# Attention scores on 32-row tiles of the array, banks shared with values' results, and a recurrent layer's weights loaded early

## The chip, the core and the metric

The kernel runs on one core of one Trainium2 chip. The core has a matrix engine (TensorE, PE in the profile), a vector engine (DVE), a scalar engine that evaluates functions (ACT), a general engine (POOL), and SyncE (SP), which here only issues transfers. Each engine works through its own instructions in order and waits on semaphores for the others. PE writes its results to PSUM, which has eight banks of 128 partitions x 512 float32 values; DVE and ACT read them from there, and POOL works on SBUF alone.

The metric is the device time of one execution in microseconds (us). Times of several runs are given as a median.

## The reference

The inputs are `x` and a context `ctx`, each 32 batches x 64 tokens x 256 features in float32. Four layers follow each other:

```
x = L0(x, ctx)        # 8 x 64-row channel attention: energies, softmax, values, 64x64 weights, relu
x = L1(x, ctx, ...)   # transformer layer: self attention, cross attention with ctx, gelu MLP
x = L2(x, ctx, ...)   # the same with other weights
x = L3(x, ctx)        # recurrent layer: token shift, mixes, decay, a scan over tokens, gate, feed-forward
```

The attention of L1 and L2 has 16 heads of 16 features:

```
scores = einsum('bhqd,bhkd->bhqk', q, k) / sqrt(16)
scores = scores * mask - 10000.0 * (1.0 - mask)
probs  = softmax(scores, axis=-1)
ctx    = einsum('bhqk,bhkd->bhqd', probs, v)
```

The MLP is `gelu(ln(x) @ w1 + b1) @ w2 + b2` with 1024 hidden features. L3 computes, for every token, `out = r @ (u * k v' + s)` and `s = k v' + w * s` on 8x8 states of 32 heads.

## The kernel before

The 2048 tokens are cut into four groups of 512 (eight batches). A group has four units of 128 tokens (two batches), numbered j = 0 to 3. All of `x` stays in SBUF.

**Order.** Each layer's work on a group is a list of small pieces with a cost (`attention`, `mlp_half`, `recurrent`). `timed` spreads a list over an interval of a made-up time axis, `emit` sorts the pieces of all lists by that time and records their instructions. The intervals come from the constants in `PARAMS`. So the cross attention of one group runs beside the projections of the next, and beside the MLP of groups that are further on. After that a scheduler of the language sets the final order of every engine's queue with its own estimate of the times; `at_once` asks it to keep a set of matmuls together. What stands in the queues is fixed from then on.

**One unit of attention** passes through these pieces (lines of the kernel before):

- `spread` (L388): eight transfers on SP's queue put the keys of a half group into `kbd`. Every head has 16 partitions, and a matmul takes 64 partitions, which hold four heads. So that each head meets only its own keys, `kbd` has four planes, and head h is non-zero in plane h % 4 alone.
- `scores` (L423): eight matmuls, for two feature halves c, two row halves r and two batches h. Each multiplies 64 rows of the transposed queries with 64 x 256 of `kbd` (4 planes x 64 keys), on a 64x64 tile of the array. The result is in two banks, one for each r. Then, for each r, DVE multiplies with the mask into SBUF (L447), POOL adds the mask's second term (L452), DVE takes the maximum over keys (L455), and DVE (r = 0) or POOL (r = 1) subtracts it (L456).
- `turn` (L459): eight transposes on PE (L467), four for each r, and ACT's exp of the turned scores (L471).
- `heads` (L473): 32 small matmuls with the values and a column of ones, into one bank `pc`. DVE takes the reciprocal of the sums (L494) and multiplies (L496) into `cn`.
- `turn_back` (L500): two transposes of `cn` into one bank `pcT`, which ACT and DVE split into a high and a low part (`split`, L179 and L180) for the output product.
- `out` (L512): the product with the output weights, added to `x` by DVE (L199).

The pieces of successive units are interleaved: scores of unit i, turn and heads of i - 1, turn_back of i - 2, out of i - 3.

**Banks.** `bank` hands out the eight banks by tag: two for products ("mm"), two for scores ("sc"), two for turned scores ("tp"), one for values' results ("pc") and one for the turned-back results ("pd"). A new tile of a tag waits until the oldest tile of that tag has been read. The MLP's output (`out_rows_of`) takes "pc" for all but the first group. Layer 0's energies take "sc" and "tp" in turn, its values "pc" and "pd". The recurrent layer uses the same pool.

**The change of phase.** Two SBUF pools of the first layers ("lw", "lp") end, and the recurrent layer's pool ("r") takes their place. Its `load` puts each weight into that pool, by default with a transfer issued on ACT's queue; `load_w` does so on SP's queue. Then the recurrent pieces start, together with the MLP of L2's later groups (`late`).

Of the kernel before, what the change touches and what calls it, by code (L numbers as in the profile page):

```python
# [23 lines left out]
P = 128  # L24
# [7 lines left out]
XM = 32  # L32
# [48 lines left out]
def tile_xattn_stack(ctx: ExitStack, tc: tile.TileContext, a: dict, out: bass.AP):  # L81
# [4 lines left out]
    small = ctx.enter_context(tc.tile_pool(name="small", bufs=4))  # L86
    psum = ctx.enter_context(tc.tile_pool(name="psum", bufs=2, space=PSUM))
    dram = ctx.enter_context(tc.tile_pool(name="dram", bufs=2, space=bass.MemoryType.DRAM))
    work = ctx.enter_context(tc.tile_pool(name="work", bufs=2))
# [4 lines left out]
    def bank(name, tag="mm"):  # L94
        return psum.tile([P, 512], FP, tag=tag, name=name, bufs=BUFS[tag])

# [130 lines left out]
    def layer0(pool):  # L227
# [32 lines left out]
        def energy(g, j):  # L260
# [3 lines left out]
            nmx = small.tile([P, 2, 2], FP, tag="nmx", name=f"nmx_{g}_{j}")  # L264
            att = pool.tile([P, 4, E], FP, tag="s", name=f"att_{g}_{j}", bufs=3)
            for h in range(2):
                pe = bank(f"pe_{g}_{j}_{h}", "sc" if v else "tp").rearrange("p (c m) -> p c m", c=2)
                hs = slice(h * S, (h + 1) * S)
                for c in range(2):
                    nc.tensor.matmul(  # L270
                        pe[:, c, :], st[g][hs, j, c * P : (c + 1) * P], kx[hs, v, :], start=True, stop=True
                    )
                nc.vector.tensor_reduce(nmx[:, h, :], pe, AX.X, ALU.max, negate=True)
                for c in range(2):
                    nc.scalar.activation(
                        att[:, 2 * h + c, :], pe[:, c, :], AF.Exp, bias=nmx[:, h, c : c + 1],
                        accum_out=rs[:, h, c : c + 1],
                    )
# [68 lines left out]
    def attention(stage, key, g, pool, ctx_of, w, mask_of):  # L347
# [75 lines left out]
        def scores(j):  # L423
            kbd, toff = st["kbd", j // 2], (j % 2) * P
            m, n = st["mask"]
            s = st["s", j] = pool.tile([P, 2, NH // 2, S], FP, tag="s", name=f"s_{tag}_{j}", bufs=3)
            banks = [bank(f"psc_{tag}_{j}_{r}", "sc") for r in range(2)]

            mms = []
            for c in (1, 0):  # L430
                for r in (1, 0):
                    rs_ = slice(r * S, (r + 1) * S)
                    for h in range(2):
                        toks = slice((2 * j + h) * S, (2 * j + h + 1) * S)
# [10 lines left out]
            for r in range(2):  # L445
                hs = slice(r * 8, r * 8 + 8)
                nc.vector.tensor_tensor(  # L447
                    s[:, r], banks[r].rearrange("p (h k) -> p h k", k=S),
                    m(j).unsqueeze(1).broadcast_to([P, 8, S]), ALU.mult,
                )  # L450
# [22 lines left out]
        def heads(j):  # L473
            pT, vts = st["pT", j], st["vts", j // 2]
            pc = bank(f"pc_{tag}_{j}", "pc")

            pcp = pc[:, : 17 * NH].rearrange("p (l n e) -> p n l e", l=2, n=8)

            mms = []
            for k in (4, 5, 6, 7, 0, 1, 2, 3):  # L480
                n = 4 * (k // 2 % 2) + 2 * (k // 4) + k % 2

# [17 lines left out]
        def turn_back(j):  # L500
            ps = bank(f"pcT_{tag}_{j}", "pd")
            for c in range(2):
# [42 lines left out]
    def mlp_half(stage, tag, g, u, w, brow):  # L545
# [337 lines left out]

    wts = {}

    with tc.tile_pool(name="lw", bufs=1) as wp, tc.tile_pool(name="lp", bufs=2) as pool:
        m1 = wp.tile([P, S], FP, name="m1")
# [152 lines left out]
        for i, L in enumerate(("L1", "L2")):  # L1040
# [29 lines left out]
    with tc.tile_pool(name="r", bufs=2, reuse_waits="tile") as pool:  # L1070
        c3 = {}

        def load(name, shape, src, eng=nc.scalar):
            c3[name] = pool.tile(shape, FP, name=name, bufs=1)
            eng.dma_start(c3[name], src)

        def load_w(*names):
            for n in names:
                load(n, [P, 2, E], a["w3"][W3[n]].rearrange("(c p) n -> p c n", p=P), nc.sync)

# [6 lines left out]

        load("mw1", [P, 2, 5 * XM], a["maa_w1"].rearrange("(c p) n -> p c n", p=P))
        load("mw2a", [P, E], a["maa_w2"][:P])
        load("mw2b", [XM, E], a["maa_w2"][P:])  # L1090
        load("step", [P, P], a["step"])
        load("st01", [P, 2, B, 2], a["st01"])
        load("dw1", [P, 2, 64], a["decay_w1"].rearrange("(c p) n -> p c n", p=P))
        hold("fx")
        hold("dfx")
        load("avg", [P, P], a["avg"])
        hold("x5", 3)
# [7 lines left out]
        hold("dx")  # L1105
        load_w("Wv", "Wr", "Wk")
        shifted_ring("vsh")

        load("sel", [P, 2, P], a["sel"])
        load("dw2", [64, E], a["decay_w2"])  # L1110
        hold("ta", 1, [P, RR + S])
# [106 lines left out]
```

## Time and profile before

| | |
|---|---|
| median of 3 runs | 1105.0 us (1099.04, 1106.01, 1105.0) |
| the profiled execution, its time | 1094.72 us |
| the profiled execution, its span on the core | 1092.9 us |
| mean granted TensorE clock in it | 0.964 |
| layer 0 | 0 to 109 us |
| L1: self attention, cross attention, rest of the MLP | 109 to 232, 232 to 347, 347 to 427 us |
| L2: self attention, cross attention | 427 to 575, 575 to 705 us |
| recurrent layer with the rest of L2's MLP | 705 to 1093 us |

How to read it: busy time is the time in which an engine executes. A row of the profile has the line of the kernel, the engine, the operation, the tile written and the tiles read, the shape, and the number of instructions; buffer numbers are left out, so `psc_L1c` stands for all score tiles of cross attention in L1, `pc_` for values' results, `ppT_` for turned scores, `pcT_` for turned-back results, `pf_` and `pfo_` for the MLP's products. A float32 matmul stands as two rows. PEld rows are weight loads, which overlap matmuls. In a timeline row the first number is the start, the second the time to the end of the last instruction of the row; brackets give idle time of that engine before it and what ended it.

### The profile page before, as it was taken

The page shows a single profiled execution, that of the slowest core. Times are in us where ns is not written, and L with a number is a line of the kernel's source. Part 1 is how long each engine was busy: PE and PEld are TensorE (multiplying, and loading weights), DVE is VectorE, ACT ScalarE, POOL GpSimd, SP SyncE. Part 2 cuts the span into 40 slices and gives each one's busy share as a digit, 9 for nine tenths or more (in the row PEclk, how much of TensorE's full clock was granted, in tenths as well). Part 3 has the DMA queues.
Part 4 walks back from the last instruction along what each step waited for, and adds up shares of the span by engine and source line. Part 5 has one row for each costly group of instructions (what it writes and reads, how often), then busy time and mean ns, then how long its engine had stood idle before and what let it go on. Part 6 is the DMA issues. An engine that isn't in the chain of part 4 may idle for free.

```text
span 1092.9 us, 26229 instructions
## 1 busy us (share of the span) xinstructions
PE 978.1 (89%) x10690; PEld 770.5 (70%) x10690; DVE 836.6 (77%) x1497; ACT 556.1 (51%) x1287; POOL 548.4 (50%) x568
## 2 busy tenths in 40 slices
PE   6898999999989999989989999889889998869757
PEld 3555776777778989877767678778678777647536
DVE  4986788777877654777688877647898987997983
ACT  4664554554556634864454455444355464346234
POOL 4354776667757344656577755434434533323300
PEclk9999999999999999989999999999999999989879
DMA  9100011111110101141111110033113121530300
GB/s 292 48 21 19 20 44 38 36 26 25 30 22 6 40 1 21 45 137 34 28 41 26 26 22 30 7 93 89 41 49 89 41 58 40 135 79 21 97 10 30
DMA packets 46364, 53.43 MB, mean 49 GB/s; under 512 B 16562, under 2 KB 40484, under 8 KB 44196
## 3 DMA queue, kind: packets, MB, share of 16 engines
q1 hardware_dynamic: 38756, 48.55, 17.0%
q10 hardware_dynamic: 7488, 3.20, 1.2%
q8 instruction: 85, 1.39, 0.5%
q14 instruction: 35, 0.29, 0.1%
HBM read 38.86 MB, written 4.21 MB: 39 GB/s over the span
## 4 chain that ended last, share of the span: by engine, by line
DVE 38%; PE 36%; ACT 8%; POOL 7%; DMA 5%; issue 4%; SPq 2%; ACTq 0%; POOLq 0%; DVEq 0%
DVE vb_r L784 6%; DVE vb_r L769 5%; PE pf_L1m L188 4%; PE pfo_L1m L188 3%; POOL s_L2c L452 2%; PE pfo_L2m L188 2%; PE pf_L2m L188 2%; DVE x L199 2%; POOL s_L1c L452 2%; SPq L392 2%; PE px_r L671 1%; DMA vb_r<-vd_r 1%; DVE x_r L675 1%; DVE s_L1c L447 1%; PE pq_L2c L188 1%
## 5 line engine op out<-in xcount | busy, mean ns | idle before, releaser
L678 POOL TENSOR_TENSOR x_r<-x_r,xn_r 128x512 f32<-128x512 f32 x40 | 60.5, 1521 | 90.9 <-DVE x_r L675 88.4
L784 DVE TENSOR_TENSOR_SCAN vb_r<-wsh,vb_r 128x512 f32<-128x512 f32 x64 | 77.0, 1260 | 5.3 <-ACT wsh L682 5.3
L188 PE MATMUL pf_L2m<-lnT_L2m,w_L 128*128 128x256 f32 x384 | 57.6, 305 | 7.1 <-DVE lnT_L2m L180 5.2
L188 PEld LDWEIGHTS pf_L2m<-lnT_L2m,w_L 128*128 128x128 f32 x384 | 51.9, 204 | 11.1 <-DVE lnT_L2m L180 5.8
L452 POOL TENSOR_TENSOR s_L1s<-s_L1s,n 128x512 f32<-128x512 f32 x32 | 42.5, 1343 | 29.0 <-DVE s_L1s L447 26.1
L452 POOL TENSOR_TENSOR s_L2s<-s_L2s,n 128x512 f32<-128x512 f32 x32 | 43.0, 1359 | 27.5 <-DVE s_L2s L447 27.4
L188 PE MATMUL pfo_L2m<-w_L,hT_L2m 128*128 128x256 f32 x384 | 55.2, 292 | 1.6 <-DVE hT_L2m L570 1.5
L452 POOL TENSOR_TENSOR s_L2c<-s_L2c,n_L2c 128x512 f32<-128x512 f32 x32 | 41.6, 1319 | 29.2 <-DVE s_L2c L447 28.2
L188 PE MATMUL pfo_L1m<-w_L,hT_L1m 128*128 128x256 f32 x384 | 54.5, 289 | 1.6 <-POOL hT_L1m L569 0.8
L188 PE MATMUL pf_L1m<-lnT_L1m,w_L 128*128 128x256 f32 x384 | 52.0, 288 | 3.9 <-ACT hf_L1m L566 1.2
L452 POOL TENSOR_TENSOR s_L1c<-s_L1c,n_L1c 128x512 f32<-128x512 f32 x32 | 41.2, 1307 | 24.3 <-DVE s_L1c L447 24.1
L188 PEld LDWEIGHTS pf_L1m<-lnT_L1m,w_L 128*128 128x128 f32 x384 | 47.6, 191 | 7.2 <-ACT hf_L1m L566 2.1
L188 PEld LDWEIGHTS pfo_L2m<-w_L,hT_L2m 128*128 128x128 f32 x384 | 48.9, 191 | 4.7 <-DVE hT_L2m L570 1.9
L188 PEld LDWEIGHTS pfo_L1m<-w_L,hT_L1m 128*128 128x128 f32 x384 | 49.3, 191 | 3.4 <-POOL hT_L1m L569 1.0
L569 POOL TENSOR_SCALAR hT_L1m<-hf_L1m 128x512 fp32r<-128x512 f32 x32 | 21.8, 682 | 55.5 <-ACT hf_L1m L566 53.8
L570 DVE TENSOR_TENSOR hT_L1m<-hf_L1m,hT_L1m 128x512 fp32r<-128x512 f32 x32 | 25.3, 791 | 30.2 <-POOL hT_L1m L569 30.1
L566 ACT ACTIVATE hf_L1m<-pf_L1m,b_L 128x256 f32<-128x256 f32 x64 | 26.6, 471 | 42.3 <-PE pf_L1m L188 39.9
L133 PE MATMUL pa_r<-vb_r,sel 128*32 128x256 f32 x256 | 22.8, 487 | 28.0 <-DVE vb_r L769 25.7
L569 POOL TENSOR_SCALAR hT_L2m<-hf_L2m 128x512 fp32r<-128x512 f32 x32 | 26.0, 816 | 43.0 <-ACT hf_L2m L566 42.9
L566 ACT ACTIVATE hf_L2m<-pf_L2m,b_L 128x256 f32<-128x256 f32 x64 | 26.6, 470 | 35.2 <-PE pf_L2m L188 27.3
L769 DVE TENSOR_TENSOR vb_r<-vb_r,ksh 128x2048 f32<-128x2048 f32 x16 | 39.3, 2468 | 6.2 <-DMA vb_r<-vd_r 6.2
L675 DVE SCALAR_TENSOR_TENSOR x_r<-px_r,vecs,sx_r 128x256 f32<-128x256 f32 x80 | 34.1, 473 | 7.2 <-PE px_r L671 6.3
(383 smaller groups left out, 3087.2 us busy)
## 6 DMA issues: line engine op xcount, KB each, us to landing
vb_r<-vd_r SPq DMA_DIRECT2D x16, 1024.0 KB
raw_w_L<-in_L_w_dram SPq DMA_DIRECT2D x4, 1024.0 KB
y<-in_y_dram SPq DMA_DIRECT2D x8, 256.0 KB
x<-in_x_dram SPq DMA_DIRECT2D x8, 256.0 KB
ctxT_L1c<-in_yT_dram SPq DMA_DIRECT2D x4, 512.0 KB
kbd<-kT_L1s SPq DMA_DIRECT2D x64, 32.0 KB
kbd<-kT_L1c SPq DMA_DIRECT2D x64, 32.0 KB
kbd<-kT_L2s SPq DMA_DIRECT2D x64, 32.0 KB
```

Source lines behind the costliest of these rows:

```text
L133: return lambda: nc.tensor.matmul(ps, sta, mov, start=start, stop=stop)
L188: nc.tensor.matmul(ps, sta[x], mov[y], start=(at == 0), stop=(at == n - 1))
L199: nc.vector.tensor_tensor(xs, xs, ps, ALU.add)
L392: nc.sync.dma_start(st["kbd", hg][hs, :, h % 4, :], st["kT"][hs, :, hg * 2 * P : (hg + 1) * 2 * P])
L452: nc.gpsimd.tensor_tensor(s[:, r], s[:, r], n(j).unsqueeze(1).broadcast_to([P, 8, S]), ALU.add)
L566: nc.scalar.activation(raw[:, i], ps[:, i], AF.Gelu_apprx_tanh, bias=w()["b1"][:, 2 * f2 + i : 2 * f2 + i + 1])
L569: nc.gpsimd.tensor_scalar(h[:, 0], raw, 1.0, 0.0, ALU.mult, ALU.add)
L570: nc.vector.tensor_tensor(h[:, 1], raw, h[:, 0], ALU.subtract)
L675: nc.vector.scalar_tensor_tensor(d[:, c], ps[:, c], vec("L3_maa_stack", 2 * m + c), sx_("x", c), ALU.add, ALU.mult)
L678: nc.gpsimd.tensor_tensor(d, d, st["x"], ALU.add)
L769: nc.vector.tensor_tensor(v, v, x.unsqueeze(1).broadcast_to([P, 4, 2 * RR]), ALU.mult)
L784: nc.vector.tensor_tensor_scan(v[:, d], flat(st["wsh"]), v[:, d], 0.0, ALU.mult, ALU.add)
```

## The change

Scores: `kbd` gets two planes, and a matmul takes 32 partitions (two heads) and 128 columns (2 planes x 64 keys). There are 16 for a unit, on 32x64 tiles, and each of the four row quarters q writes a bank of its own. The two banks of q = 2, 3 are one tile of tag "b", those of q = 0, 1 one of tag "a", with one buffer each. The mask's multiply reads two banks in one instruction.

Banks: "sc", "pc" and "pd" go. Values' results (`heads`) take the first bank of an "a" tile, turned-back results (`turn_back`) that of a "b" tile; so "a" and "b" each serve scores and results in turn. Layer 0's energies of a unit take one "a" or "b" tile, its values "tp". The MLP's output takes "tp" before the recurrent phase and "pc" in it, for all but the first group. The recurrent layer gets a PSUM pool of its own with the old tags.

Weights: twelve of the recurrent layer's arrays are loaded by `load_early` into the pool that lasts for the whole kernel, at time 4.0 of the made-up axis, on SP's queue. The other six stay at the change of phase, all on SP's queue. The kernel is built with `dynamic_dma_scratch_size=1024`.

```diff
+    def two_banks(name, tag):
+        return psums["two"].tile([P, 2, 512], FP, tag=tag, name=name, bufs=1)
...
+            pes = two_banks(f"pe_{g}_{j}", "ab"[v])
             for h in range(2):
-                pe = bank(f"pe_{g}_{j}_{h}", "sc" if v else "tp").rearrange("p (c m) -> p c m", c=2)
+                pe = pes[:, h].rearrange("p (c m) -> p c m", c=2)
...
-            pr = bank(f"pr_{g}_{j}", "pc" if j % 2 else "pd")
+            pr = bank(f"pr_{g}_{j}", "tp")
...
-                    st["kbd", hg][hs, :, h % 4, :], st["kT"][hs, :, hg * 2 * P : (hg + 1) * 2 * P]
+                    st["kbd", hg][hs, :, h % 2, :], st["kT"][hs, :, hg * 2 * P : (hg + 1) * 2 * P]
...
-            banks = [bank(f"psc_{tag}_{j}_{r}", "sc") for r in range(2)]
+
+            banks = [two_banks(f"psc_{tag}_{j}_{r}", "ab"[r])[:, :, :256] for r in range(2)]
 
             mms = []
             for c in (1, 0):
-                for r in (1, 0):
-                    rs_ = slice(r * S, (r + 1) * S)
+                for q in (3, 2, 1, 0):
+                    qs = slice(q * 32, (q + 1) * 32)
                     for h in range(2):
                         toks = slice((2 * j + h) * S, (2 * j + h + 1) * S)
                         ktoks = slice(toff + h * S, toff + (h + 1) * S)
                         mms.append(mm(
-                            banks[r][h * S : (h + 1) * S, c * 256 : (c + 1) * 256].rearrange(
-                                "p (i k) -> p i k", i=4),
-                            st["qT"][rs_, c, toks], kbd[rs_, c, :, ktoks],
+                            banks[q // 2][h * S : (h + 1) * S, q % 2, c * P : (c + 1) * P].rearrange(
+                                "p (i k) -> p i k", i=2),
+                            st["qT"][qs, c, toks], kbd[qs, c, :, ktoks],
                         ))
...
-            pc = bank(f"pc_{tag}_{j}", "pc")
+            pc = two_banks(f"pc_{tag}_{j}", "a")[:, 0]
...
-            ps = bank(f"pcT_{tag}_{j}", "pd")
+            ps = two_banks(f"pcT_{tag}_{j}", "b")[:, 0]
...
-                st["ps"] = bank(f"pfo_{tag}", "pc" if g else "mm").rearrange("p (j n) -> p j n", j=2)
+                st["ps"] = bank(f"pfo_{tag}", ("pc" if stage == 5 else "tp") if g else "mm").rearrange(
+                    "p (j n) -> p j n", j=2)
...
+    def load_to(pool, name, shape, src):
+        c3[name] = pool.tile(shape, FP, name=name, bufs=1)
+        nc.sync.dma_start(c3[name], src)
+
+    def load_early():
+
+        load_to(const, "step", [P, P], a["step"])
+        load_to(const, "mw1", [P, 2, 5 * XM], a["maa_w1"].rearrange("(c p) n -> p c n", p=P))
+        load_to(const, "st01", [P, 2, B, 2], a["st01"])
+        load_to(const, "mw2a", [P, E], a["maa_w2"][:P])
+        load_to(const, "mw2b", [XM, E], a["maa_w2"][P:])
+        for n in ("Wv", "Wr", "Wk"):
+            load_to(const, n, [P, 2, E], a["w3"][W3[n]].rearrange("(c p) n -> p c n", p=P))
+        load_to(const, "dw1", [P, 2, 64], a["decay_w1"].rearrange("(c p) n -> p c n", p=P))
+        load_to(const, "dw2", [64, E], a["decay_w2"])
+
+        load_to(const, "sel", [P, 2, P], a["sel"])
+        load_to(const, "avg", [P, P], a["avg"])
...
-        env["kbds"] = ring(wp, "kbd", [P, 2, 4, GR // 2], 3, blank)
+        env["kbds"] = ring(wp, "kbd", [P, 2, 2, GR // 2], 3, blank)
...
+        plan.append([(4.0, load_early)])
         emit(*plan)
...
-        def load(name, shape, src, eng=nc.scalar):
-            c3[name] = pool.tile(shape, FP, name=name, bufs=1)
-            eng.dma_start(c3[name], src)
+        def load(name, shape, src):
+            load_to(pool, name, shape, src)
```

More of the change, by code (lines that the diff above doesn't have):

```diff
@@ L87, in tile_xattn_stack @@
     psum = ctx.enter_context(tc.tile_pool(name="psum", bufs=2, space=PSUM))
+    psums = {"mm": psum}
     dram = ctx.enter_context(tc.tile_pool(name="dram", bufs=2, space=bass.MemoryType.DRAM))
@@ L94, in bank @@
     def bank(name, tag="mm"):
-        return psum.tile([P, 512], FP, tag=tag, name=name, bufs=BUFS[tag])
+        return psums[tag].tile([P, 512], FP, tag=tag, name=name, bufs=BUFS[tag])
+    def two_banks(name, tag):
+        return psums["two"].tile([P, 2, 512], FP, tag=tag, name=name, bufs=1)
     x_rows = a["x"].rearrange("(g j p) n -> g p j n", g=NG, p=P)
@@ L447, in scores @@
                 nc.vector.tensor_tensor(
-                    s[:, r], banks[r].rearrange("p (h k) -> p h k", k=S),
-                    m(j).unsqueeze(1).broadcast_to([P, 8, S]), ALU.mult,
+                    s[:, r].rearrange("p (q h) k -> p q h k", q=2), banks[r].rearrange("p q (h k) -> p q h k", k=S),
+                    m(j).unsqueeze(1).unsqueeze(1).broadcast_to([P, 2, 4, S]), ALU.mult,
                 )
@@ L474, in heads @@
             pT, vts = st["pT", j], st["vts", j // 2]
-            pc = bank(f"pc_{tag}_{j}", "pc")
+            pc = two_banks(f"pc_{tag}_{j}", "a")[:, 0]
             pcp = pc[:, : 17 * NH].rearrange("p (l n e) -> p n l e", l=2, n=8)
             mms = []
-            for k in (4, 5, 6, 7, 0, 1, 2, 3):
-                n = 4 * (k // 2 % 2) + 2 * (k // 4) + k % 2
+            for k in (6, 7, 0, 1, 2, 3, 4, 5):
+                n = 4 * (k % 2) + k // 2
                 for q in range(4):
@@ L881, in recurrent @@
         return first, second, third
-    wts = {}
-    with tc.tile_pool(name="lw", bufs=1) as wp, tc.tile_pool(name="lp", bufs=2) as pool:
+    wts, c3 = {}, {}
+    def load_to(pool, name, shape, src):
[13 more added lines that the diff above has]
+        load_to(const, "avg", [P, P], a["avg"])
+    with (
+        tc.tile_pool(name="lw", bufs=1) as wp, tc.tile_pool(name="lp", bufs=2) as pool,
+        tc.tile_pool(name="psum_l", bufs=2, space=PSUM) as pp,
+    ):
+        psums["two"] = psums["tp"] = pp
         m1 = wp.tile([P, S], FP, name="m1")
@@ L1065, in tile_xattn_stack @@
             plan.append([(load, load_mlp("L2"))] if i == 0 else [(MLP_LOAD, load_mlp("L1"))])
+        plan.append([(4.0, load_early)])
         emit(*plan)
-    with tc.tile_pool(name="r", bufs=2, reuse_waits="tile") as pool:
-        c3 = {}
-        def load(name, shape, src, eng=nc.scalar):
-            c3[name] = pool.tile(shape, FP, name=name, bufs=1)
-            eng.dma_start(c3[name], src)
+    with (
+        tc.tile_pool(name="r", bufs=2, reuse_waits="tile") as pool,
+        tc.tile_pool(name="psum_r", bufs=2, space=PSUM, reuse_waits="tile") as pp,
+    ):
+        for tag in ("sc", "tp", "pc", "pd"):
+            psums[tag] = pp
+        def load(name, shape, src):
+            load_to(pool, name, shape, src)
         def load_w(*names):
             for n in names:
-                load(n, [P, 2, E], a["w3"][W3[n]].rearrange("(c p) n -> p c n", p=P), nc.sync)
+                load(n, [P, 2, E], a["w3"][W3[n]].rearrange("(c p) n -> p c n", p=P))
         def hold(tag, bufs=2, shape=None):
@@ L1086, in shifted_ring @@
             c3[name] = ring(pool, name, [P, 2, RB, S], 2, lambda t: nc.gpsimd.memset(t[:, :, :, 0], 0.0))
[L1088 to L1093, printed above, removed]
         hold("fx")
         hold("dfx")
-        load("avg", [P, P], a["avg"])
         hold("x5", 3)
@@ L1105, in tile_xattn_stack @@
         hold("dx")
-        load_w("Wv", "Wr", "Wk")
         shifted_ring("vsh")
-        load("sel", [P, 2, P], a["sel"])
-        load("dw2", [64, E], a["decay_w2"])
         hold("ta", 1, [P, RR + S])
@@ L1206 @@
     from concourse.bass_utils import run_bass_kernel_spmd
-    nc = bacc.Bacc("TRN2", target_bir_lowering=False, num_devices=1)
+    nc = bacc.Bacc("TRN2", target_bir_lowering=False, num_devices=1, dynamic_dma_scratch_size=1024)
     arrays, aps = {}, {}
```

## The prediction

> **What bounds the kernel now.** I read the page's head and chain first, then busy time by stage, then the score blocks on the timeline, and last the change of phase near 710 us.
>
> ```profile
> span 1092.9 us, 26229 instructions
> ...
> PE 978.1 (89%) x10690; PEld 770.5 (70%) x10690; DVE 836.6 (77%) x1497; ACT 556.1 (51%) x1287; POOL 548.4 (50%) x568
> ...
> DVE 38%; PE 36%; ACT 8%; POOL 7%; DMA 5%; issue 4%; SPq 2%; ACTq 0%; POOLq 0%; DVEq 0%
> ```
>
> PE is nearly full, yet the chain that ended last is shared between DVE and PE. The stages differ: the two transformer layers run from 109 to 705 us, the recurrent layer from 705 on, with its DVE scans setting the pace from 760. One steady group of cross attention (busy time in a window):
>
> ```profile
> core 0: us, PE busy (x) PEld busy (x) DVE busy (x) ACT busy (x) POOL busy (x), PEclk, DMA share, GB/s
> 260.40:288.40 28.00, 25.37 (x445) 20.04 (x444) 23.78 (x50) 14.68 (x39) 20.37 (x20) 1.00 0.13 30
> ```
>
> Of 28.0 us PE is busy 25.4, idle 2.6, and DVE is busy 23.8, or 85%. Taking work off PE helps only as long as DVE, which serves its queue in order, answers in time.
>
> **Scores on PE.** The timeline of PE shows two forms of one unit's scores (128 queries):
>
> ```profile
> 235.88 1.11 PE L133 MATMUL psc_L1c<-kbd,qT_L1c 64*64 64x256 f32 x16
> 236.91 1.70 PE L188 MATMUL po_L1s<-wo_L,cT_L1s 128*128 128x256 f32 x12
> ...
> 239.94 1.08 PE L133 MATMUL psc_L1c<-kbd,qT_L1c 64*64 64x256 f32 x8
> 240.95 1.09 PE L467 MATMUL ppT_L1c<-ident,s_L1c 128*128 128x128 f32 x8
> 241.97 1.08 PE L133 MATMUL psc_L1c<-kbd,qT_L1c 64*64 64x256 f32 x8
> ```
>
> A whole unit (8 matmuls, two rows each, on four 64x64 tiles) takes 1.03 us to the start of the next work. Half a unit, on only two tiles, takes 1.01. So tiles do run side by side, and a block costs its rows per tile: four of 0.215 us each, and about 0.17 to get going. Adding up, along the timeline, the time from every scores row to the next start on PE gives 22.8, 19.8, 22.3 and 19.8 us for L1s, L1c, L2s, L2c: 84.6 us.
>
> The change has 16 matmuls of 128 columns on eight 32x64 tiles. A tile still sees four rows, of 128 columns; the transposes' rows of 128 columns start 0.109 us apart. A block is then 4 x 0.109 + 0.17 = 0.60 us. But the built program splits nearly every unit: its halves wait for different banks, and PE's order holds 121 blocks, 114 of them halves and 7 whole. A half costs as much as a whole, so the stages need 121 x 0.60 = 72.6 us: **-12.0**. In a steady group, where units were whole, it is even a loss (four at 1.03 against eight at 0.60); the gain comes from units that were cut up before. Bounds: -14.5 if a block starts 0.02 us sooner; +40 if 32-row tiles do not overlap, which no row shows either way (a half would cost 1.03).
>
> [...]
>
> Values' results lose nothing and stand together: before, five of 64 blocks were cut by scores, costing some 1.7 us over the usual 0.70 each: **-1.7** (0 to -2).
>
> **What the sharing costs.** Before, a unit's scores needed only the multiply of the unit before (L447). Now bank pair "a" passes from the scores' first half (r = 0) to values' results and back, "b" from the second half to the turned-back results. In the new DVE order the reciprocal and normalising product (L494, L496), which free "a", stand behind the maximum and subtraction of the scores just made. So a loop closes through POOL. Its rows, from the steady group's timelines of DVE and POOL:
>
> ```profile
> 261.55 1.29 DVE L447 TENSOR_TENSOR s_L1c<-psc_L1c,m_L1c 128x512 f32<-128x512 f32 x2 [0.16 <-PE psc_L1c L133]
> ...
> 265.04 0.65 DVE L455 TENSOR_REDUCE mx_L1c<-s_L1c 128x8 f32<-128x512 f32 x1
> ...
> 265.70 0.23 DVE L494 RECIPROCAL ris_L1c<-pc_L1c 128x16 f32<-128x16 f32 x1
> 265.84 0.63 DVE L456 TENSOR_TENSOR s_L1c<-s_L1c,mx_L1c 128x512 f32<-128x512 f32 x1
> 266.38 0.41 DVE L496 TENSOR_TENSOR cn_L1c<-pc_L1c,ris_L1c 128x256 f32<-128x256 f32 x1
> ```
> ```profile
> 262.32 2.54 POOL L452 TENSOR_TENSOR s_L1c<-s_L1c,n_L1c 128x512 f32<-128x512 f32 x2 [5.29 <-DVE s_L1c L447]
> 264.81 1.05 POOL L456 TENSOR_TENSOR s_L1c<-s_L1c,mx_L1c 128x512 f32<-128x512 f32 x1
> ```
>
> One multiply 0.68, POOL's add 1.28, maximum 0.65, reciprocal 0.23, subtraction 0.63, product 0.41: 3.9 us, 4.3 with handovers of about 0.1, 5.4 where POOL first subtracts for the other half (1.05). Against that, the work in the new PE order between one first half and the next, priced by rows of before, is 5.35, 5.15, 6.85 and 5.75 us in a steady group of L1c. The cover is just enough, with no other DVE row in front. Likewise from a first half to its turn: 3.7 us needed (multiply, add, maximum, subtraction), while the PE work between has a median of 5.4 us over the 64 units, 17 of them under 4.4. It was 8.2, never below 5.05. The same multiply stood 1.0 to 2.1 us late behind other DVE rows in the steady units of before (scores ending at 265.69, 270.12 and 275.25, multiply at 266.71, 271.55 and 277.31), which cost nothing then.
>
> I put the new waits at 1.0 us a group: the shortfalls of 0.05 and 0.25 us, and one DVE row of 0.68 in front once. 16 groups: **+16**. Lower bound 0 (2.6 us of idle already in each group may absorb them). Upper bound: the 32 shorter units each 1.1 us late (a chain of 5.2, as 3.7 plus a wait of 1.5, against 4.1): +35.
>
> **Table loads.** Where MLP and attention overlap, the ACT order swaps exp and gelu more often: 61 table loads for 47, each 1.28 us (group L471, L566), 18 us in all. ACT is half idle there (40.7 busy of 80 us from 347 to 427), and PE has MLP products between. I take **+2**; 0 to +8, a quarter to a half of the loads uncovered.
>
> [...]
>
> **Early weights.** At the change of phase (timelines of ACT and PE, then the chain):
>
> ```profile
> 716.48 1.10 ACT L156 ACTIVATE xn_r<-x,nmr_r,rstd_r 128x256 f32<-128x256 f32 x2 [6.82 <-DMA dw<-in_decay_w_dram]
> ```
> ```profile
> 717.13 0.33 PE L164 MATMUL pln_r<-ident,xn_r 128*128 128x128 f32 x1 [3.58 <-ACT xn_r L156]
> ```
> ```profile
> 708.82 2.41 DMA mw<-in_maa_w_dram
> ...
> 711.25 4.03 DMA Wo<-in_w_dram
> ```
>
> ACT issues ten transfers in a row, each waiting for an earlier one, and the first norm stands behind them. In the new order none is on ACT: the norm follows the second gelu pair directly. Next late are PE's own MLP products (717 to 760 is all but full), so the gain is PE's idle, 3.58 + 0.45: **-4**, 0 (if x of the MLP is late) to -6.8 (all of ACT's wait). The recurrent layer starts that much sooner, and its DVE pace carries it to the end. The last six transfers stay, now all on SP. The twelve early ones stand on SP behind the first layer's MLP weights, issued at 18.9 us; SP's next issue was at 38.2. Twelve issues of 0.47 are 5.6 us, and 1.5 MB at the 291 GB/s of that stretch 5.4 us: hidden by that gap, and would cost up to 5 if the cross weights behind them were needed before 45 us (they wait for DVE's split first).
>
> **Smaller edits.** kbd's planes: the same 64 transfers of 32 KB a stage, the blanks half as long on POOL before they are needed: 0. Layer 0's energies share one two-bank tile per unit, and the new order has the second half wait for ACT's exps of the first (0.68 + 1.35 us); 2.7 us of other PE work stand between: 0, -1 to +4. MLP outputs on the two "tp" banks: fewer clashes with values, more with turns: 0, -2 to +2.
>
> **Sum**, against the profiled execution (span 1092.9, its time 1094.7): -12.0 - 1.7 + 16 + 2 - 4 = +0.3, so 1095. The median of the runs, 1105.0, is 0.9% above that execution; scaled, I forecast **1106**.
>
> **Rivals.** (1) *The loop stays covered*: waits 0, tables 0: -17.7, at 1077, scaled **1087**. For: the scheduler laid the order out with these bank waits known to it; the lengths just fit. Against: DVE at 85%. (2) *The bank loop decides*: waits of +35 in place of +16: 1114, scaled **1125**, slower. Place: L494 and L496 behind L455 on DVE. It decides once waits exceed 27 us, 0.42 us a unit. For: the 1.0 to 2.1 us lateness of the multiply. Against: DVE empties its queue while PE waits. (3) *32-row tiles do not run side by side*: 121 x 1.03 = 125 us, +52 on the forecast: **1158**. The 64-row tiles speak against it.
>
> **Chances.** Forecast 0.37, (1) 0.28, (2) 0.31, (3) 0.04. A measurement of this kernel can tell about 1%, 11 us: the forecast's own range is 1094 to 1116. Faster 0.28, same 0.37, slower 0.35. The range takes in (1) down to 1084 and (2) up to 1132.
>
> **What would show it.** Scores blocks of 0.60 us on 32x64 tiles, their total near 73 us; at 1.03, (3) holds. PE's idle before scores and turns (waiting for L496 and L456) from 109 to 705 us: grown by some 16 us, or not at all, or by 35. 61 table loads. No ACT wait before the first xn_r. Wrong would be a price for POOL's rows or DVE's that moves with the new order, or a recurrent layer that lengthens for reasons of its own order.

## The result: 3.8% slower

| | before | changed |
|---|---|---|
| median of six runs each | 1102.3 us (1098.2 to 1109.6) | 1145.1 us (1139.7 to 1150.2) |
| ratio to before, 95% interval | 1 | 1.0383 (1.0346 to 1.0421) |
| profiled execution, its time and its span | 1094.7, 1092.9 us | 1139.7, 1137.9 us |
| mean granted TensorE clock in it | 0.964 | 0.955 |

The forecast was 1106 us with a range up to 1132: wrong, and on the side of the rival "the bank loop decides" (1125), only worse.

**The profile after.** First the page's head and the shares of the chain that ended last, of the changed kernel:

```profile
span 1137.9 us, 28316 instructions
...
PE 1001.8 (88%) x11714; PEld 795.4 (70%) x11714; DVE 841.2 (74%) x1497; ACT 576.2 (51%) x1301; POOL 536.6 (47%) x568
...
DVE 36%; PE 35%; POOL 10%; ACT 7%; issue 5%; DMA 4%; SPq 2%; ACTq 0%; POOLq 0%; DVEq 0%
```

PE was to be relieved, and is busy 24 us longer than before; POOL's share of the chain went from 7 to 10%.

**Where the 45 us are.** The chain says little when everything is spread over it, so I cut the span in three, at the first scores row of L1 and at the first norm of the recurrent layer, and added up PE's timeline in each part: from the start of each matmul row to the next start, or to its own end if PE then idles. Of the time in which the clock was granted at half, half is booked as lost to the clock.

| us | before | changed | difference |
|---|---|---|---|
| layer 0 | 109.1 | 120.6 | **+11.5** |
| L1 and L2 | 608.1 | 635.8 | **+27.7** |
| - scores on PE | 81.5 | 73.5 | -8.0 |
| - values' results on PE | 47.2 | 45.6 | -1.6 |
| - all other rows on PE | 424.3 | 437.6 | +13.3 |
| - lost to the half clock | 11.6 | 18.6 | +7.0 |
| - PE idle | 43.5 | 60.6 | +17.1 |
| recurrent phase | 375.8 | 381.5 | +5.7 |

The last row is hardly the change's: over all profiles of this study, with nearly one and the same order in that phase, it lies between 375.8 and 383.7 us.

**Layer 0** is read in the timeline of PE, before and then after, at one place of a group:

```profile
72.75 2.10 PE L270 MATMUL pe<-kx,y 64*128 64x256 f32 x16
```
```profile
79.09 1.13 PE L275 MATMUL pe<-kx,y 64*128 64x256 f32 x4
...
81.24 1.13 PE L275 MATMUL pe<-kx,y 64*128 64x256 f32 x4
...
83.19 1.13 PE L275 MATMUL pe<-kx,y 64*128 64x256 f32 x4
```

Before, the two halves of a unit's energies (64 rows of the array each) stood next to each other and ran side by side: 16 rows, two units, in 2.10 us. After, one half stands alone and takes 1.13 us for 4 rows. A half costs what a unit did; PE's time for `pe` rose from 22.1 to 34.5 us. The halves came apart because both now lie in one tile: the second half's products wait until ACT's exp has read the first's. Where no other work fills that time, PE idles for it:

```profile
30.63 1.13 PE L275 MATMUL pe<-kx,y 64*128 64x256 f32 x4 [1.76 <-ACT att L280]
```

**Scores and their neighbours.** One half of a unit, in the changed kernel's steady cross attention:

```profile
662.40 0.67 PE L137 MATMUL psc_L2c<-kbd,qT_L2c 32*64 32x128 f32 x16
663.00 0.97 PE L192 MATMUL po_L2c<-wo_L,cT_L2c 128*128 128x256 f32 x6
...
666.99 0.48 PE L192 MATMUL po_L2c<-wo_L,cT_L2c 128*128 128x256 f32 x2
...
671.54 0.74 PE L192 MATMUL po_L2c<-wo_L,cT_L2c 128*128 128x256 f32 x4
```

The block starts its successor 0.60 us later, just as forecast. But look at the output product: in one piece it takes 0.97 us to its end, cut in two by other work 0.48 + 0.74 = 1.22. By the starts of single rows, a row of an output product takes 0.120 us among its like, 0.209 us when a scores or values block follows, and 0.223 us right behind one. So a block costs some 0.2 us more in its neighbours' rows. Blocks of scores and values, counted as one where they touch, rose from 118 to 161 in L1 and L2. Of the 13.3 us by which all other rows grew, 7.7 stand in the rows next to such a block, near 0.2 for each new one, and 4.6 in rows next to an idle gap, which belong to the waits. A new stretch of any other kind costs less: on PE the stretches of one tile rose from 617 to 679 here, and in e14 below to 654, where these other rows grew by 1.6 us only.

**One steady group**, the second of a stage, from its first values block to the next group's, as busy time in a window. First L1's cross attention before and after, then L2's:

```profile
272.14:300.09 27.95, 25.32 (x441) 20.01 (x440) 23.78 (x50) 14.62 (x38) 20.37 (x20) 1.00 0.14 31
297.24:328.52 31.28, 27.62 (x506) 21.47 (x505) 25.30 (x49) 14.73 (x39) 20.02 (x20) 1.00 0.14 28
```
```profile
615.20:644.66 29.46, 26.78 (x442) 20.90 (x441) 23.15 (x46) 14.61 (x38) 19.07 (x18) 0.94 0.11 24
652.54:682.76 30.22, 27.50 (x505) 21.38 (x505) 23.61 (x44) 14.74 (x39) 19.42 (x19) 1.00 0.11 24
```

In L1 the group takes 31.3 us for 28.0: PE is busier by 2.3, as these units were whole before and are halves now, and idles 1.0 us more (3.7 for 2.6), which is what the prediction put for a group. In L2 it is 30.2 for 29.5, part of the latter at half clock. The second groups of the self attentions even became shorter (29.3 for 29.8 us, and 28.1 for 36.2, the latter in part at half clock), so the steady group does not tell the whole: in windows of the same kind, the first and the third group of the four stages grew by some 23 us each, summed over the stages, and what lies outside these three became 14 us shorter.

### The profile page after: what moved, and what is told of

The parts are those of the page before. It is cut to its first block, busy times and chain, and to the rows that moved or that the text cites. A ratio compares the mean times of both kernels' runs of the same rounds, so it can differ in the third digit from the quotient of the medians.

```text
span 1137.9 us, 28316 instructions
## 1 busy us (share of the span) xinstructions
PE 1001.8 (88%) x11714; PEld 795.4 (70%) x11714; DVE 841.2 (74%) x1497; ACT 576.2 (51%) x1301; POOL 536.6 (47%) x568
## 4 chain that ended last, share of the span: by engine, by line
DVE 36%; PE 35%; POOL 10%; ACT 7%; issue 5%; DMA 4%; SPq 2%; ACTq 0%; POOLq 0%; DVEq 0%
DVE vb_r L791 6%; DVE vb_r L776 4%; PE pfo_L1m L192 3%; PE pf_L1m L192 3%; SPq L397 2%; PE pe L275 2%; PE pfo_L2m L192 2%; POOL s_L2s L458 2%; DVE x L203 2%; POOL s_L1s L458 1%; PE pf_L2m L192 1%; PE px_r L678 1%; POOL s_L2c L458 1%; DVE x_r L682 1%; DVE s_L2s L453 1%
## 5 line engine op out<-in xcount | busy, mean ns | idle before, releaser
L458 POOL TENSOR_TENSOR s_L1s<-s_L1s,n 128x512 f32<-128x512 f32 x32 | 41.7, 1307 | 42.5 <-DVE s_L1s L453 35.9
L192 PE MATMUL pfo_L1m<-w_L,hT_L1m 128*128 128x256 f32 x384 | 56.8, 293 | 5.2 <-DVE hT_L1m L576 3.5
L458 POOL TENSOR_TENSOR s_L1c<-s_L1c,n_L1c 128x512 f32<-128x512 f32 x32 | 42.3, 1323 | 38.6 <-DVE s_L1c L453 23.9
L458 POOL TENSOR_TENSOR s_L2c<-s_L2c,n_L2c 128x512 f32<-128x512 f32 x32 | 43.4, 1357 | 35.3 <-DVE s_L2c L453 30.2
L458 POOL TENSOR_TENSOR s_L2s<-s_L2s,n 128x512 f32<-128x512 f32 x32 | 42.5, 1331 | 34.1 <-DVE s_L2s L453 25.3
L192 PE MATMUL pfo_L2m<-w_L,hT_L2m 128*128 128x256 f32 x384 | 56.0, 293 | 1.1 <-POOL hT_L2m L575 0.7
L137 PE MATMUL pa_r<-vb_r,sel 128*32 128x256 f32 x256 | 23.2, 494 | 27.7 <-DVE vb_r L776 25.3
L280 ACT ACTIVATE att<-pe,nmx 128x256 f32<-128x256 f32 x64 | 29.8, 473 | 30.2 <-DVE nmx L278 24.7
L575 POOL TENSOR_SCALAR hT_L1m<-hf_L1m 128x512 fp32r<-128x512 f32 x32 | 21.7, 680 | 47.9 <-ACT hf_L1m L572 45.6
L572 ACT ACTIVATE hf_L2m<-pf_L2m,b_L 128x256 f32<-128x256 f32 x64 | 26.5, 472 | 32.4 <-PE pf_L2m L192 28.9
L572 ACT ACTIVATE hf_L1m<-pf_L1m,b_L 128x256 f32<-128x256 f32 x64 | 26.6, 473 | 30.5 <-PE pf_L1m L192 30.4
```

The source lines that it names most:

```text
L137: return lambda: nc.tensor.matmul(ps, sta, mov, start=start, stop=stop)
L192: nc.tensor.matmul(ps, sta[x], mov[y], start=(at == 0), stop=(at == n - 1))
L280: nc.scalar.activation(att[:, 2 * h + c, :], pe[:, c, :], AF.Exp, bias=nmx[:, h, c : c + 1], accum_out=rs[:, h, c : c + 1],)
L458: nc.gpsimd.tensor_tensor(s[:, r], s[:, r], n(j).unsqueeze(1).broadcast_to([P, 8, S]), ALU.add)
L572: nc.scalar.activation(raw[:, i], ps[:, i], AF.Gelu_apprx_tanh, bias=w()["b1"][:, 2 * f2 + i : 2 * f2 + i + 1])
L575: nc.gpsimd.tensor_scalar(h[:, 0], raw, 1.0, 0.0, ALU.mult, ALU.add)
```

## The experiments

All ratios are to the kernel before on the same chip, with 95% intervals. "Layers" is the length of L1 and L2 as above, "scores", "idle" and "clock" are PE's times in it.

| run | ratio | layers | scores | idle | clock |
|---|---|---|---|---|---|
| before | 1 | 608.1 | 81.5 | 43.5 | 11.6 |
| changed | 1.038 (1.035 to 1.042) | 635.8 | 73.5 | 60.6 | 18.6 |
| e1 pairs in layer 0 | 1.031 (1.027 to 1.034) | 639.2 | 73.3 | 58.7 | 22.4 |
| e2 early loads alone | 0.996 (0.994 to 0.999) | 604.3 | 82.4 | 41.5 | 10.1 |
| e3 no early loads | 1.045 (1.040 to 1.050) | 643.5 | 73.4 | 62.8 | 22.3 |
| e4 sharing at 64 rows | 1.022 (1.019 to 1.025) | 633.4 | 116.3 | 35.8 | 5.0 |
| e5 first half leads | 1.032 (1.027 to 1.037) | 639.3 | 48.4 | 91.9 | 21.4 |
| e6 values off a | 1.019 (1.015 to 1.023) | 628.0 | 41.7 | 78.3 | 35.2 |
| e7 e6, MLP in mm | 1.026 (1.020 to 1.032) | 636.1 | 42.6 | 90.5 | 30.5 |
| e8 turned-back off b | 1.052 (1.047 to 1.058) | 660.9 | 73.1 | 76.8 | 31.3 |
| e9 e4, first half leads | 1.032 (1.027 to 1.037) | 644.9 | 75.3 | 72.3 | 15.9 |
| e10 e6 with 64 rows | 1.026 (1.022 to 1.030) | 632.8 | 68.2 | 73.2 | 20.5 |
| e11 e2 and pairs | 0.996 (0.993 to 0.999) | 608.4 | 81.0 | 42.4 | 14.9 |
| e12 copy frees a | 1.026 (1.021 to 1.031) | 636.1 | 58.4 | 71.6 | 26.7 |
| e13 copy frees tp | 1.025 (1.021 to 1.029) | 636.4 | 42.5 | 85.5 | 33.1 |
| e14 before, other order | 1.009 (1.006 to 1.013) | 620.4 | 82.5 | 51.9 | 13.4 |
| e15 before, other order 2 | 1.015 (1.011 to 1.019) | 631.1 | 81.2 | 56.1 | 21.6 |
| e16 scores twice | 1.118 (1.113 to 1.123) | 733.2 | 78.7 | 128.6 | 55.2 |

### The parts one by one: e1 to e4

**e1**, in the changed kernel:

```diff
-            for h in range(2):
-                pe = pes[:, h].rearrange("p (c m) -> p c m", c=2)
-                hs = slice(h * S, (h + 1) * S)
-                for c in range(2):
+            pe2 = [pes[:, h].rearrange("p (c m) -> p c m", c=2) for h in range(2)]
+            for c in range(2):
+                for h in range(2):
+                    hs = slice(h * S, (h + 1) * S)
                     nc.tensor.matmul(
...
+            for h in range(2):
+                pe = pe2[h]
                 nc.vector.tensor_reduce(nmx[:, h, :], pe, AX.X, ALU.max, negate=True)
```

> The changed kernel, with layer 0's four energy products of a unit issued ahead of both maxima, so that both halves (rows 0-63 and 64-127 of the array) run side by side again. Theory: of the 43 us lost, 11.5 are layer 0's, because the two halves of a unit no longer stand together (34.5 us of PE for the energies against 22.1 before). Then pe is back near 22 us, the first scores start near 109 us instead of 120.6, and the time is 1145 - 11 = 1134. Rival: layer 0 is late through the early loads on SP or the waits for ACT; then the first scores stay near 120 us and the time near 1145.

Measured: 1134.3 us, 10.8 less than the changed kernel by the medians and 8.6 by the ratios; `pe` 17.6 us, the first scores at 113.2 us. So layer 0's loss is mostly the lost pairing, and not the loads. (In e4, where each half keeps a bank and a tile of its own, `pe` takes 21.9 us.) In the profiled executions 7.4 of the 11.5 us come back; the rest stays as waits (layer 0's idle rose from 9.1 to 15.9 us).

**e2**, the kernel before with `load_early`, the other six loads on SP and `dynamic_dma_scratch_size=1024`, all as in the change's diff.

> The kernel before with nothing but the recurrent layer's twelve early loads (and the smaller scratch memory that makes room for them). The prediction's term: -4 us, 0 to -6.8, so 1098 (ratio 0.996), with no ACT wait of 6.8 us ahead of the first xn_r. Rival: the gain is swallowed by the MLP's own products or the recurrent layer's vector work, 1102 (1.000); or the twelve loads delay the first layer's weights, up to +5 (1107).

Measured: 1098.7 us, 0.996. The timeline of ACT around the change of phase:

```profile
710.97 0.84 ACT L566 ACTIVATE hf_L2m<-pf_L2m,b_L 128x256 f32<-128x256 f32 x2 [0.90 <-PE pf_L2m L188]
711.70 1.09 ACT L156 ACTIVATE xn_r<-x,nmr_r,rstd_r 128x256 f32<-128x256 f32 x2
```

The norm follows the gelu pair with no wait, where 6.82 us stood. The interval excludes "no change" only just, and the medians on that chip lie 1.8 us apart.

**e3**, the changed kernel without the early loads (`load` and its twelve calls as before).

> The changed kernel with the twelve loads put back to the start of the recurrent layer, as before. If the early loads are worth 4 us here too: 1149. If they were lost in the longer attention stages: 1145. If they made layer 0 late: less than 1145, with the first scores earlier than 120 us.

Measured: 1149.4 us, 1.045. That agrees with the same 4 us here, though the two intervals overlap; and layer 0 (120.9 us long without the early loads) is not their doing.

**e4**, the kernel before with its two score banks named one by one and shared (PSUM pools by phase, as in the change):

```diff
-            banks = [bank(f"psc_{tag}_{j}_{r}", "sc") for r in range(2)]
+            banks = [bank(f"psc_{tag}_{j}_{r}", ("sa", "sb")[r]) for r in range(2)]
...
-            pc = bank(f"pc_{tag}_{j}", "pc")
+            pc = bank(f"pc_{tag}_{j}", "sa")
...
-            ps = bank(f"pcT_{tag}_{j}", "pd")
+            ps = bank(f"pcT_{tag}_{j}", "sb")
```

> The kernel before, scores on 64-row tiles and two banks as before, but the two score banks are named one by one and shared: values' results take the first half's bank, the turned-back results the second's; layer 0 as before. Theory: the sharing is what costs. Its built order has 111 score stretches where 78 stood, nearly all halves; at 1.01 us each that is 112 us of PE for the scores where 84.6 were, and some 15 us of new waits: 1102 + 42 = 1144 (ratio 1.038). Rival: the sharing is covered and the 32-row tiles with their many blocks are what costs; then the scores stay below 90 us and the time near 1105 (1.003).

Measured: 1124.2 us, 1.022. Half right. The scores take what was said (116.3 us), yet there is no new wait: PE's idle is lower than before. So sharing, without any 32-row tile but with the new order that comes with it, costs 24 us, near the 20 by which the rival "the bank loop decides" stood over the median. But it is not clear from this run whether PE's 35 us more for cut units cost that, or whether PE only filled a time that the loop sets. The next runs ask that.

### Does PE's time for scores count: e5, e9, e16

**e5** is e1 with the order of the strips turned, so that a unit starts with the pair that comes free last and stays whole:

```diff
-                for q in (3, 2, 1, 0):
+                for q in (1, 0, 3, 2):
```

> The pairs restored in layer 0 as in the first experiment, the bank sharing unchanged, and one edit more: a unit's scores start with the strips of bank pair a, the pair that comes free last, so that the built order has 67 score stretches where 119 stood. Theory 1 (the cut units are what costs): scores 64 x 0.69 = 44 us where 75.3 were, and some 50 crossings between tile shapes fewer, 0.19 us each: 1134 - 31 - 10 = 1093, less any new wait, so 1093 to 1105. Theory 2 (the loop through bank a decides, whatever PE does): PE's idle grows by what the scores save, 1134 within 6.

Measured: 1136.9 us for 1134.3: theory 2. The scores lost 25 us of PE's time and the time did not move; PE's idle grew by 33 us (the neighbours gained, too). Who ends PE's waits, in e5:

```profile
PE ppT_L1s L475 <- DVE s_L1s L464: 6.8, 7, 1.7
PE pc_L1c L137 <- DVE s_L1c L455: 4.5, 4, 1.4
```

(tile waited for by PE, the releaser with its line, us in all, times, longest.) L464 is the subtraction ahead of the turn, L455 the multiply that must empty bank pair a before values can have it.

**e9** does the same to e4 (`for r in (0, 1)` in place of `(1, 0)`).

> The sharing at 64 rows (e4, 1124 us, 117 us of PE for cut scores) with the scores of a unit starting in the first half's bank, the one that comes free last: 69 stretches in the built order. If PE's time for the halves is what e4 lost: scores near 70 us, time 1124 - 25 = 1099. If the loop through the shared bank is what it lost, and PE only filled the time: 1124 within 5, PE's idle up by the 40 us that the scores save.

Measured: 1136.5 us for 1124.2. 41 us less for scores, 36 us more idle, and 11 us more of half clock: slower than either expectation. So PE's time for cut units is not what held e4, unless the new order brought a cost of its own. It may have: in e5 and e9 the half that could start first now stands behind the half that waits longest for its bank, so these two runs do more than take work off PE. The comparison of e6 and e10 below is free of that.

**e16** is e5 with the list of a unit's products given twice: `at_once(mms + mms)`.

> e5 (sharing, whole units, 1136.9 us) with a unit's score products all issued twice into the same banks; the result is the same, the work of PE for scores doubles, from 50 us to some 90. If PE's time counts: 1137 + 40 = 1177. If the bank loop decides and PE only waits in it: 1137 within 8, with the idle of 92 us down to 60 and less time at half clock.

Measured: 1231.3 us: both expectations missed. PE does 30 us more for scores, and the layers take 94 us more, with 37 us more idle and 34 us more lost to the half clock. Values now wait longer for the multiply of the next scores:

```profile
PE pc_L1c L137 <- DVE s_L1c L455: 12.9, 5, 3.0
PE pc_L1s L137 <- DVE s_L1s L455: 9.6, 1, 9.6
PE pc_L2c L137 <- DVE s_L2c L455: 9.2, 5, 3.2
```

This points to PE's time for scores being on the loop after all (scores, multiply, values in one bank pair) when it is long, while the short blocks of e5 are covered by other work. The run also changed the order of everything else, and I can't say how much of the 94 us that is.

### The banks: e6, e7, e8, e10

**e6** is e1 with `pc = bank(f"pc_{tag}_{j}", "tp")`: values' results off bank pair a.

> As the first experiment, but values' results go to the two tp banks and no longer share bank pair a; the turned-back results still share b. The built order has 63 score stretches. Theory 1: scores near 44 us, crossings saved as in the run before, and the loop gone with its waits (some 15 us of the idle): 1134 - 31 - 10 - 15 = 1078 to 1095. Theory 2: the same, since the loop is gone, but only through idle. A rival to both: turns and values now wait for each other in the tp banks, or VectorE becomes the bound, and the time stays above 1115.

Measured: 1120.7 us, 1.019: 14 us better than e1, and far from 1078 to 1095, on the side of the rival that was named. The scores are whole and take 41.7 us, but PE idles 78 us and loses 35 to the half clock: its waits for VectorE rose from 30 us in e1 to 45, those for ScalarE from 20 to 29. The timeline of PE in e6, and below it busy time in four windows of 3.41 us, on the grid on which the clock changes:

```profile
293.75 0.47 PE L192 MATMUL pq_L1c<-hi_L1c,wx_L 128*128 128x512 f32 x1 [1.64 <-DVE lo_L1c L184]
295.39 0.50 PE L192 MATMUL pq_L1c<-lo_L1c,wx_L 128*128 128x512 f32 x1 [1.17 <-DVE lo_L1c L184]
295.73 0.64 PE L192 MATMUL pq_L1c<-hi_L1c,wx_L 128*128 128x512 f32 x2
...
297.73 1.06 PE L192 MATMUL pq_L1c<-hi_L1c,wx_L 128*128 128x512 f32 x2
```
```profile
289.59:293.01 3.42, 2.52 (x79) 2.00 (x77) 2.69 (x8) 3.25 (x7) 1.84 (x3) 1.00 0.28 58
293.01:296.42 3.41, 1.49 (x5) 1.05 (x6) 3.08 (x8) 1.02 (x3) 3.41 (x5) 1.00 0.15 31
296.42:299.84 3.42, 3.42 (x10) 2.60 (x9) 0.61 (x2) 0.69 (x1) 3.32 (x3) 0.50 0.00 0
299.84:303.25 3.41, 3.41 (x114) 2.89 (x113) 1.29 (x2) 1.73 (x4) 1.15 (x1) 1.00 0.14 38
```

Two waits of 1.64 us (in part in the window ahead) and 1.17 us leave PE busy for 1.49 us of a window, and in the next window the granted clock is 0.50: the same two rows take 1.06 us instead of 0.64. The wait is paid once as idle time and once more, 1.7 us, by the work behind it.

**e7** is e6 with the MLP's output in "mm" in place of "tp".

> As the run before, and the MLP's outputs in the mm banks, not tp. If the tp banks are what waits now: 3 to 10 us less than the run before. If not: within 4 us of it.

Measured: 1130.4 us, 10 us worse than e6, and neither of the two expectations. Taking the MLP out of the tp banks gains nothing; as it crowds the mm banks instead, the run does not tell whether it waited in tp.

**e8** is e1 with `ps = bank(f"pcT_{tag}_{j}", "tp")`: the turned-back results off b, values still in a.

> As the first experiment, but it is the turned-back results that go to the tp banks, and values' results still share bank pair a. The built order still has 116 score stretches. Theory 1: no gain, 1134 within 8, scores near 74 us. If sharing as such costs in either bank: about half of what the run without values in a gains.

Measured: 1158.6 us, 1.052, the worst layout, and 24 us above e1 where no change or a gain was expected. The units stay cut (73.1 us), as was said. In the self attentions the turns now wait 11.9 us for VectorE's subtraction, where 2.0 us are listed in e1; what makes it late is not shown.

**e10** is e6 with `scores`, `kbd` and the order of heads as in the kernel before, so with 64-row tiles.

> e6 (values' results in the tp banks, 1120.7 us) with its scores put back on four 64x64 tiles and keys in four planes; banks, loads and layer 0 unchanged. The built order has 63 score stretches in both. If PE's time counts: scores 64 x 1.03 = 66 us where 44.7 were, so 1121 + 21 = 1142. If it doesn't, and what the 32-row tiles save only becomes idle time and half clock: 1121 within 8.

Measured: 1132.2 us, 1.026. This lies between the two expectations. By the medians the 32-row tiles are worth 11.5 us here, 8 by the ratios, whose intervals overlap. In the profiled executions only 4.8 us of it lie in L1 and L2, where the scores are, for 26.5 us less of PE's time: the half clock takes back 14.7 and idle 5.

### What holds the banks, and the order itself: e12 to e15, e11

**e12** and **e13** are e1 and e6 with a copy that frees the bank of values' results sooner:

```diff
-            pcv = pc[:, : 17 * NH].rearrange("p (h e) -> p h e", e=17)
+            pcs = small.tile([P, 17 * NH], FP, tag="pcs", name=f"pcs_{tag}_{j}", bufs=2)
+            nc.scalar.copy(pcs, pc[:, : 17 * NH])
+            pcv = pcs.rearrange("p (h e) -> p h e", e=17)
```

> The first experiment (pairs in layer 0, 1134 us, sharing as in the changed kernel) with a copy by ScalarE of values' results from the bank to memory, so that bank pair a comes free after the copy and not after VectorE's reciprocal and product, which stand behind the next unit's maximum and subtraction. The built order then has 92 score stretches for 119. If that end of the loop (L494 and L496 of before) is what decides: 10 to 25 us less, 1109 to 1124. If the other end decides (values wait for the multiply of the next scores, which POOL's and VectorE's queues hold): within 5 of 1134. ScalarE's copies themselves cost nothing on the path, as it is half idle.

> e6 (values' results in the tp banks, 1120.7 us) with the same copy. If the turns wait for values' results to leave the tp banks behind VectorE's queue: 10 to 20 us less, 1101 to 1111, and PE's idle from layer 1 to the change of phase (78 us in e6) down to 60. If not: within 5 of 1121.

Measured: 1131.0 us (3 less than e1, within the intervals) and 1130.4 us (10 more than e6, where less or no change was expected). The copy does free the bank sooner: in e12 it ends 0.5 to 1.5 us behind a unit's last values product (medians of the four stages), where the product of e1 ended 2.3 to 2.5 us behind it. So the reciprocal and the product behind VectorE's queue do not look like what the loop turns on; my place for the price was wrong.

**e14** and **e15** change nothing but the order of a unit's score products in the kernel before: `for r in (0, 1)`, and `for c in (0, 1)`. Banks, tiles and loads stay.

> The kernel before, banks, tiles and loads unchanged; only a unit's scores start with the strips of the first half, as in e9. It moves some 320 of 1740 rows on PE and as many on VectorE. If the time is a matter of the particular order the scheduler finds, this neutral edit costs 10 us or more: 1112 or above. If it is the shared and crowded banks that cost: within 6 of 1101.

> The kernel before with the two column halves of a unit's scores in the other order, nothing else: some 220 rows moved on PE, 180 on VectorE. As for e14: 1112 or above if the order found decides, within 6 of 1101 if the banks do.

Measured: 1111.7 and 1118.4 us, 1.009 and 1.015. An edit that adds no work moves an eighth to a fifth of PE's queue and gives 10 to 16 us away, as idle time and half clock again (8 to 13 us and 2 to 10 us).

**e11** is e2 with layer 0's products ahead of both maxima, as in e1.

> The kernel before with the early loads (e2, ratio 0.996) and layer 0's four energy products of a unit issued ahead of both maxima; banks as before. Layer 0's energies took 22.1 us of PE where e1's order took 17.6, so up to 4 us off e2: 1095 (0.993). If layer 0 is bound by VectorE and ScalarE (17.3 and 11 to 17 us of 20 busy), nothing: 1098.5 (0.996).

Measured: 1098.8 us, 0.996, the same as e2. `pe` took 19.2 us for 21.4, and layer 0's length went from 110.3 to 108.2 us, which the time does not show. e2 and e11 are the only versions that beat the kernel before, by 0.4%.

## Why the prediction was wrong

Term by term, with the step of the prediction and what stands in its place:

- **Scores, -12.0: measured -8.0.** The blocks are what was said (120 of 0.61 us, 73.5 for 72.6), and the tiles run side by side, so rival 3 falls. The 84.6 us to compare with held 3 us of half clock, which I had counted as work.
- **A block priced at 0.60 us and no more: this step failed.** The 0.17 us that a block takes to get going is one part; another 0.2 us a block stand in the rows ahead of and behind it, for which the sum has no term. The number of blocks speaks against the change with more weight than I gave it: 7.7 us over 43 new blocks of scores and values. This alone eats most of the 9.6 us gained on scores and values.
- **Values, -1.7: measured -1.6.**
- **Waits, +16: PE's idle +17.1, and with the early loads' 4 us taken out about +21,** to which the 4.6 us in rows next to idle gaps may be added. The size was near, the place wrong. PE's waits for DVE hardly grew (28.4 to 29.9 us in L1 and L2), those for ACT did (9.4 to 20.8), and those without a visible cause (0.2 to 6.1); and in e12 freeing bank a ahead of L494 and L496 gains 3 us, which is within the intervals. Nothing of the new waits can be pinned on one row.
- **The half clock, no term: +7.0.** I had taken a wait at its own length.
- **Table loads, +2**: 61 of 1.28 us, as said. PE's idle gaps that a table load overlaps grew from 0.9 to 5.3 us, so the term is at most 4.4; no run takes it apart.
- **Early weights, -4: agrees.** e2 measured 0.4%, its interval just clear of no change; e3 points the same way, with intervals that overlap.
- **Layer 0, 0 (up to +4): measured +11.5. This step failed worst.** I priced the wait of the second half and found 2.7 us of other work to hide it. I did not ask what else the wait does: it parts two halves that ran side by side, and a half alone costs what the pair did. Earlier in the prediction the same fact was read from the scores' own rows ("a half costs as much as a whole").

The prediction's frame was at fault as well: a sum of terms on PE. In the stages with attention PE's time does not count one to one: 25 us less of it in e5 gave nothing and 41 us less in e9 made it slower (in an order that brought waits of its own), 26.5 us less in e6 than in e10 gave 4.8 in these layers, and 30 us more in e16 went with 94. The forecast of no change rested on a gain of 14 us against a loss of 16; these runs suggest that most of the gain was not there to be had.

**What stays open** is how the 28 us of the layers divide between the shared banks and the order that the scheduler finds. With the shared pair, five orders (e1, e4, e5, e9, e12) give 1.022 to 1.032. With the banks of before, three orders (before, e14, e15) give 1.000 to 1.015. The groups don't overlap, so the banks most likely cost something: 0.7% lie between the best of the one and the worst of the other, some 2% between the middles. So few orders give no firm bound. That the kernel before has the best order of its three is likely to be part of the 28 us, and no fault of the change's idea.

## What to carry to other kernels

When a program's edit gives two pieces that run side by side one common tile, look in the new order for whether they still stand together: the price of a wait can be hidden and the price of the parting not (layer 0 grew by 11.5 us here, and e1 brought 7.4 of them back). Count the blocks on small tiles of the array, not only the time in them, since each new one cost its neighbours 0.2 us here; and expect to pay a wait on PE up to twice if it leaves PE idle for more than half of a 3.41 us window: here 75 of 116 windows with PE busy for 40 to 50%, and all 225 below that, were followed by one at half clock, and in e6 such a one cost 1.7 us. Before crediting work taken off an engine, ask whether idle time would take its place: a run that adds or removes that work, with the order kept as far as can be, tells it.

## What the runs showed of the hardware

**The granted clock follows PE's idle time, window by window.** In all 18 profiles of this study the clock is either full or half and changes on a grid of 3.413 us. Of the windows at full clock, all 225 in which PE was busy for less than 40% were followed by one at half clock; of those with 40 to 50%, 75 of 116; with 50 to 60%, 52 of 154; with 60 to 80%, 28 of 674; above 80%, none of 4093. From half clock it came back only after a window in which PE was busy for 80% or more.

The gaps in the windows that led to half clock were mostly shorter than a window: the median of the longest one, as far as it lies in such a window, is 1.9 us, and in 300 of 392 changes to half clock no gap that touched that window was as long as 3.4 us. A window with 60% of it idle, in one piece or several, always led to half clock (225 of 225), and one with about half of it idle, 40 to 60%, about every second time (127 of 270).
